# A two-layer graph network on one core: the prologue's folding and index work placed behind layer 0's table, three more superchunks gathered in place

## The chip, the cores and the metric

One Trainium2 chip, one of its cores. The metric is the device time of one execution in microseconds (us), the median of the runs. The engines are TensorE (PE, its weight loads PEld), VectorE (DVE), ScalarE (ACT), GpSimd (POOL) and SyncE (SP); "PEq", "SPq" and the like are their sequencers. The instructions of one engine stand in the trace in the order in which the program issues them.

## The reference, cut to what matters

6250 nodes with 256 features, 200,000 edges sorted by their destination. The features are normalized and cut at zero, run through two layers of graph attention (4 heads, then 1), and added to the input. One layer, in short:

```python
hx = (x @ Wg).reshape(n, h, f)
te = relu(edge_attr @ We + be) * exp(x @ Wo + bo)[src][:, None]   # edges, and a self loop of each node
he = (te @ Wge).reshape(-1, h, f)
al = leaky_relu((hx*a_s).sum(-1)[src] + (hx*a_d).sum(-1)[dst] + (he*a_e).sum(-1), 0.2)
al = exp(al - segment_max(al, dst)[dst])
al = al / segment_sum(al, dst)[dst]
out = segment_sum(hx[src] * al[:, :, None], dst) + b
```

Layer 0 is `relu(out + x)`, layer 1 `out + x`, and the result is the input plus all this.

## The kernel before, in words

**Tables and superchunks.** For each layer a table T in DRAM holds one row per node: hx, its two attention terms, the gate exp(x @ Wo + bo), and in layer 0 the two numbers of the node's normalization. The attention vectors are folded into the weights first (`fold`, lines 186 to 199; `fold_e`, lines 201 to 214, for the edges): TensorE turns a weight matrix, ScalarE copies it out of PSUM (line 183), TensorE multiplies it with the vectors (193, 208), VectorE copies the columns into the weights (197, 198, 210, 213). The edges go in 66 superchunks per layer, 64 of them of 24 chunks of 128 edges. A superchunk's source rows are gathered from T by 24 indirect DMAs, which POOL issues (line 941), into a buffer G of 128 x 24 x 270. VectorE makes logits, running maxima over each destination and weights, scales the rows (1303 in layer 0; ScalarE does it in layer 1, 1312), and TensorE sums them by destination with one-hot matrices (1322).

**Buffers.** Superchunk k takes the buffer k mod 3 as a new tile, whose first gather waits until the tile before in this place has been read entirely. The exception is superchunk 3: `own` (lines 692, 693) gives it superchunk 0's tile G0 itself, and each gather then waits for the readers of its own column only. Superchunk 0 has no gathers from T: its 24 columns of input rows are gathered from x during the prologue (line 274) and go through the same steps as the table's tiles.

**The prologue** (lines 218 to 439) makes layer 0's table in 49 tiles of 128 nodes (NT), in nine groups of 2, 5, 7, 7, 7, 7, 7, 5 and 2 (`g0` is 9), and then the 24 columns of superchunk 0 as groups 9 (6 columns) and 10 (18). The order of all work is written out by hand in one loop over k. In round k stand: `turn` of tile k+1 (two products with the identity on TensorE, line 342, a copy on ScalarE, 344), `norm` of tile k+3 (ScalarE, 336), up to four pieces of statistics by `step`, `keep` of tile k-1 (VectorE adds the bias and writes the row, 474), and `mult` of tile k (TensorE, 470). At the first norm of a group `drain` issues what its statistics still lack.

**Statistics** (`stats`, lines 283 to 325): per tile a bn_stats (291) and a bn_aggr (294) on VectorE, then per group variance plus epsilon (299), a first guess of the inverse root (301), minus half the variance (303), and three Newton steps, which VectorE makes in nine pieces or POOL in twelve instructions and three that write the result (307 to 324). Groups 3 to 9 use POOL.

**What else the rounds hold:** `more` loads layer 1's weights (round 5), the index loads (round 6) and the index work (`indices`, 476 to 573, and `index_group`, 629 to 675; 33 pieces, nearly all VectorE's, one every other round from round 17 and one each from 50), the folds at rounds 12 to 14 (edges, layer 0), 24 to 26 (layer 1) and 30 to 32 (edges, layer 1), and one gather of x in rounds 0 to 9 and in every fourth from 16. `idle` (254) multiplies the identity with itself, 128 x 512, and is used three times at the start. The group's rows go to T in `store` (357 to 362): two small ScalarE instructions and a DMA on SP's queue. Behind the last store `load_lb`, `load_ea` and `load_fl` issue superchunk 0's edge inputs; `lb` is a copy of `locrow`, which the index work writes to DRAM (520), and `fl` of `flags` (538).

**The edge loop** (`edges`, 678 to 774) starts with `nodes`, which loads rows of T and x into `tw`, then `gather`, `spread` (1065, 1066: it compares `lb`), `parts`, and the rest of superchunk 0.

**SP's queue.** The program gives the DMAs of SP and ScalarE eight semaphores in turn: a DMA is issued only when the one eight before it has landed, and all behind it on the queue wait with it.

Of the kernel before, what the change touches and what calls it, by code (L numbers as in the profile page):

```python
# [31 lines left out]
P = 128  # L32
# [47 lines left out]
class Kernel:  # L80
# [137 lines left out]
    def prologue(self):  # L218
# [7 lines left out]
        with ExitStack() as c:  # L226
# [56 lines left out]
            def stats(g):  # L283

                n, x = len(groups[g]), xs[g]
                w = GT if g < g0 else C
                st = wp.tile([P, w, 6], F32, name=f"st{w}", bufs=2 if g < g0 else 1)
                mv = wp.tile([P, w, 2], F32, name=f"mv{w}", bufs=3 if g < g0 else 1)
                s = wp.tile([P, 3, w], F32, name=f"sc{w}", bufs=3 if g < g0 else 1)
                for i in range(n):  # L290
                    V.bn_stats(st[:, i, :], x[:, i, :])
                    yield
# [12 lines left out]
                e = nc.gpsimd if 3 <= g <= g0 else V  # L305
# [59 lines left out]
            ahead = {g: stats(g) for g in range(1, len(groups))}  # L365
# [4 lines left out]
            def step(g):  # L370

                for q in list(ahead):
                    if q > g if q < g0 else k < (16 if q == g0 else NT):
                        continue
# [7 lines left out]
            for k in range(-3, len(tiles) + 1):  # L382
                if k == 6:
                    next(index)
                    gi = self.index_load(0, wp)
                    index = chain(index, self.index_group(0, wp, gi))
                if k > 16 and k % 2 or k > NT:
                    next(index, None)
                if k == 5:
                    more()  # L390
                if k == 8:
# [5 lines left out]
                if k in (12, 24, 30):  # L397
                    folds.append(fold(self.L[1], pt) if k == 24 else fold_e(self.L[k // 30], pt))
                    next(folds[0])
                if k in (14, 26, 32):  # L400
                    drain(folds.pop())
                if k == 26:
                    edge_weights(self.L[1])
                if 0 <= k + 1 < len(tiles):
# [10 lines left out]
                if 0 <= k - 1 < len(tiles):  # L415
# [7 lines left out]
                if 0 <= k < 10 or k >= 14 and k % 4 == 0:  # L423
                    next(rows0, None)
                if k == max(NT - 6, 7):
                    while not hasattr(self, "flags"):
                        next(index)
                    next(index)
                if 0 <= k < len(tiles):
                    mult(*tiles[k])  # L430
                while kept < g0 and groups[kept][-1] <= k - (3 if k < NT - 3 else 1):
                    store(kept)
                    kept += 1
                    if kept == g0:
                        self.load_lb(0)
                        self.load_ea(0)
                        self.load_fl(0)
# [240 lines left out]
    def edges(self, ctx):  # L678
# [13 lines left out]
        if len(steps) > 3 and steps[3]["L"].l == 0:  # L692
            steps[3]["own"] = self.G0
# [16 lines left out]
        for k, st in enumerate(steps):  # L710
# [13 lines left out]
            if st["s"] + 3 == self.NS:  # L724
                self.ending(st, *steps[k + 1:k + 3], pv, late, steps[k + 3] if k + 3 < len(steps) else None)
                pv = late = None
                continue
            self.gather(nx)
# [946 lines left out]
```

## Time and profile before

| | us |
|---|---|
| median of 3 runs | 4016.55 |
| lowest, highest | 4015.93, 4017.98 |
| the profiled execution | 4015.31 |
| its span, first to last instruction | 4013.5 |

| engine | busy us | share of the span |
|---|---|---|
| TensorE | 2655.2 | 66% |
| VectorE | 2446.4 | 61% |
| ScalarE | 1119.4 | 28% |
| POOL | 2998.9 | 75% |

A timeline row gives start, length, engine, line, operation, tiles written and read with their shapes, how many alike, and in brackets the idle time before with what ended it. A group's row gives the same with the sum of busy time, the mean length of one in ns, and the sum of the idle time before them. The DMA-issuing instructions of POOL are counted as busy.

### The profile page before, as it was taken

Reading aid. Unit: us, or ns where it says so; the run is one execution under the profiler, and the core shown is the slowest. Engines: PE = TensorE matmul, PEld = TensorE weight load, DVE = VectorE, ACT = ScalarE, POOL = GpSimd, SP = SyncE. Lnnn points to the kernel's source line nnn. Section 1 sums busy time; section 2 is a strip of 40 time slices with the busy share of each in tenths; the row PEclk is TensorE's granted clock in tenths of the full one; section 3 lists DMA queues with packets and bytes.
Section 4 is the critical chain, followed back from the end, with each engine's and each line's share of the span. In section 5 each row is a group of like instructions: output and inputs, shape, how many; then the busy total and the mean of one; then the engine's idle time right before and its main releaser. Section 6 shows DMA issues by size and latency. Waiting matters only on the chain.

```text
span 4013.5 us, 37615 instructions
## 1 busy us (share of the span) xinstructions
PE 2655.2 (66%) x9998; PEld 1744.1 (43%) x9998; DVE 2446.4 (61%) x6071; ACT 1119.4 (28%) x2676; POOL 2998.9 (75%) x3264
## 2 busy tenths in 40 slices
PE   8776766766766666666676566566665665665665
PEld 6454444444444444444454343343343343343343
DVE  7898877877877877877874443443443443443445
ACT  6211111111111111111124343343443443443441
POOL 6777777777777777777767777777777777777775
PEclk9888887788888888888888777777777777777777
DMA  7555555555555555555555445445445545545543
GB/s 245 141 160 151 145 154 144 150 154 144 152 154 145 150 154 144 151 155 143 152 155 145 133 138 143 134 137 145 137 134 143 139 132 144 138 132 143 140 131 94
DMA packets 240037, 584.66 MB, mean 146 GB/s; under 512 B 64843, under 2 KB 97265, under 8 KB 239579
## 3 DMA queue, kind: packets, MB, share of 16 engines
q0 software_dynamic: 150144, 422.75, 39.6%
q1 hardware_dynamic: 89133, 159.15, 12.4%
q8 instruction: 86, 1.41, 0.1%
q14 instruction: 130, 1.06, 0.1%
q10 hardware_dynamic: 544, 0.28, 0.0%
HBM read 544.19 MB, written 38.12 MB: 145 GB/s over the span
## 4 chain that ended last, share of the span: by engine, by line
POOL 32%; DVE 28%; issue 14%; PE 11%; ACT 9%; DMA 7%; DVEq 0%; SPq 0%; POOLq 0%; ACTq 0%
POOL G L941 31%; DVE G L1303 8%; ACT G L1312 7%; DMA G<-T,src 7%; PE y L1041 4%; PE u L1322 4%; DVE S L1132 4%; DVE lb L1065 2%; PE ps L470 1%; DVE m L1251 1%; ACT R L1042 1%; DVE rt L1181 1%; DVE al L1199 1%; DVE al L1197 1%; DVE fb L1212 1%
## 5 line engine op out<-in xcount | busy, mean ns | idle before, releaser
L941 POOL DMA_INDIRECT G<-T,src x3102 | 2945.2, 949 | 961.5 <-issue 910.7
L1322 PE MATMUL u<-G,S 128*128 128x270 f32 (+1 forms) x6252 | 1578.4, 415 | 193.3 <-DVE G L1293 190.1
L1322 PEld LDWEIGHTS u<-G,S 128*128 128x128 f32 x6252 | 1284.6, 207 | 487.5 <-DVE G L1293 217.0
L1312 ACT ACTIVATE G<-G,kw 128x256 f32<-128x256 f32 x1512 | 609.0, 497 | 0.0
L1042 ACT ACTIVATE R<-y,webd 128x1024 f32<-128x1024 f32 (+2 forms) x264 | 235.4, 892 | 1275.9 <-PE y L1041 791.4
L1219 PE MATMUL lf<-ident,fb 128*36 128x128 f32 (+1 forms) x132 | 49.6, 376 | 757.5 <-DVE fb L1212 755.6
L1195 DVE TENSOR_TENSOR G<-rt,G 128x96 f32<-128x96 f32 (+1 forms) x132 | 30.4, 230 | 804.7 <-DMA G<-T,src 804.3
L1303 DVE TENSOR_TENSOR G<-G,kps 128x6144 f32<-128x6144 f32 (+3 forms) x77 | 440.9, 5735 | 0.0
L1132 DVE TENSOR_TENSOR S<-kps,loc 128x3072 f32<-128x3072 f32 x132 | 437.7, 3316 | 4.6
L1041 PE MATMUL y<-ea,webd 64*128 64x256 f32 (+1 forms) x1056 | 391.1, 835 | 50.0 <-ACT R L1042 50.0
L1050 PE MATMUL zad<-R,wea 128*64 128x384 f32 (+1 forms) x1056 | 297.6, 704 | 158.6 <-ACT R L1042 158.3
L1219 PEld LDWEIGHTS lf<-ident,fb 128*36 128x36 f32 (+1 forms) x132 | 15.7, 119 | 798.0 <-DVE fb L1212 795.5
L1050 PEld LDWEIGHTS zad<-R,wea 128*64 128x64 f32 x1056 | 85.8, 183 | 420.9 <-ACT R L1042 338.9
L1327 ACT ACTIVATE U<-u 128x270 f32<-128x270 f32 (+1 forms) x132 | 51.8, 393 | 636.8 <-PE u L1322 636.8
L1354 DVE SCALAR_TENSOR_TENSOR mg<-U,mw 128x1 f32<-128x1 f32 x66 | 14.7, 223 | 281.2 <-ACT mw L1352 281.2
L1041 PEld LDWEIGHTS y<-ea,webd 64*128 64x128 f32 x1056 | 123.7, 286 | 122.4 <-ACT R L1042 68.4
L1285 DVE SCALAR_TENSOR_TENSOR G<-U,kw,G 1x257 f32<-1x257 f32 x62 | 29.5, 476 | 183.4 <-ACT G L1312 183.4
L470 PE MATMUL fin<-wg,h1T 128*128 128x260 f32 x264 | 127.6, 634 | 4.3 <-ACT h1T L1417 4.3
L1181 DVE STREAM_TRANSPOSE rt<-zad 128x768 f32<-128x768 f32 (+1 forms) x130 | 126.1, 970 | 4.4 <-PE zad L1167 4.4
L1153 PE MATMUL zad<-a,Q 128*128 128x12 bf16 (+1 forms) x132 | 25.9, 196 | 148.6 <-DVE a L1148 148.2
L1065 DVE TENSOR_TENSOR lb<-lb,kps 128x1536 bf16<-128x1536 bf16 (+1 forms) x68 | 113.0, 1661 | 0.0
L1427 ACT ACTIVATE t1row<-t1row 128x1 f32<-128x1 f32 x66 | 13.4, 203 | 347.1 <-DVE t1row L474 347.1
(225 smaller groups left out, 2303.2 us busy)
## 6 DMA issues: line engine op xcount, KB each, us to landing
G<-T,src POOLq DMA_INDIRECT x3102, 2.8
ea<-in_ea_dram SPq DMA_DIRECT2D x64, 768.0 KB
lb<-locrow SPq DMA_DIRECT2D x64, 384.0 KB
nd<-t1row SPq DMA_DIRECT2D x66, 225.8 KB
tw<-nd SPq DMA_DIRECT2D x66, 225.8 KB
tw<-T SPq DMA_DIRECT2D x66, 117.2 KB
T<-t1row SPq DMA_DIRECT2D x66, 113.8 KB
tw<-in_x_dram SPq DMA_DIRECT2D x66, 112.0 KB
```

The source lines that it names most:

```text
L470: self.nc.tensor.matmul(ps[:, :L.MW], hT[:, k, :], self.wg[L.l][:, k, :], start=(k == 0), stop=(k == 1))
L941: nc.gpsimd.indirect_dma_start(out=G[:, c, 0:L.TW], out_offset=None, in_=self.T[L.l][0:self.N, :], in_offset=bass.IndirectOffsetOnAxis(ap= ...
L1041: nc.tensor.matmul(y[:, i, :n], self.webd[l][r, :], ea[r, w], start=True, stop=True)
L1042: nc.scalar.activation(R[:, :, w], y[:, :, :n], AF.Relu, bias=self.be[l])
L1050: nc.tensor.matmul(st["zad"][i * PH:(i + 1) * PH, o], self.wea[l][0], R[:, i, w], start=True, stop=False)
L1065: V.tensor_tensor(lb[:, :, :n], lb[:, :, :n], self.k_part.unsqueeze(2).to_broadcast([P, i, n]), op=OP.is_equal)
L1132: nc.vector.tensor_tensor(st["S"][:, c0:c1, :], self.k_iota.unsqueeze(1).to_broadcast(w), self.loc[:, o + c0:o + c1].unsqueeze(2).to_broad ...
L1181: V.transpose(rv[:, :32 * c].rearrange("p (b n) -> p b n", b=2), z.rearrange("p (b n) -> p b n", b=2)[:, :, :16 * c])
L1219: self.nc.tensor.transpose(self.lf[0:e.shape[1], 1:P + 1], e, self.ident)
L1303: nc.vector.tensor_tensor(v, v, pw[:, c0:c1, :].unsqueeze(3) .to_broadcast([P, c1 - c0, H, L.F]), op=OP.mult)
L1312: self.nc.scalar.activation(v, v, AF.Copy, scale=st["w"][:, c:c + 1])
L1322: nc.tensor.matmul(st["u"][:, :L.W], S[:, i, :], G[:, i, 0:L.W], start=(j == 0), stop=(j == c - 1))
```

## The change

- The five identity products `idle(5)` stand in round 1, ahead of tile 2's turn.
- `stats` takes several groups at once: 7, 8 and 9 (thirteen tiles) share their Newton steps. POOL makes them for groups 2 to 7 instead of 3 to 9.
- The gathers of x beyond the first six come one in every other round, from the round after group 2's statistics are issued.
- Group 10's statistics may begin in round 45 instead of 49.
- The index loads move from round 6 to 20, `tw`'s from 8 to 23, `more` from 5 to 26. The index work begins in round 51, one piece per round; what is left is issued behind the last round.
- The three folds move to rounds 53, 56 and 61 (f = 4, 7, 12, counted from the table's end).
- The table's last rows are kept and stored first thing in round 49; `load_ea` follows there, `load_lb` and `load_fl` in round 61.
- Superchunks 3, 4 and 5 of layer 0 are gathered into the tiles of superchunks 0, 1 and 2 themselves.

```diff
@@ -280,16 +280,17 @@
             for _ in range(6):
                 next(rows0, None)
-            def stats(g):
-
-                n, x = len(groups[g]), xs[g]
-                w = GT if g < g0 else C
-                st = wp.tile([P, w, 6], F32, name=f"st{w}", bufs=2 if g < g0 else 1)
-                mv = wp.tile([P, w, 2], F32, name=f"mv{w}", bufs=3 if g < g0 else 1)
-                s = wp.tile([P, 3, w], F32, name=f"sc{w}", bufs=3 if g < g0 else 1)
-                for i in range(n):
-                    V.bn_stats(st[:, i, :], x[:, i, :])
-                    yield
+            def stats(*gs):
+
+                n, g = sum(len(groups[g]) for g in gs), gs[0]
+                w = GT if n <= GT else C
+                st = wp.tile([P, w, 6], F32, name=f"st{w}", bufs=2)
+                mv = wp.tile([P, w, 2], F32, name=f"mv{w}", bufs=3 if w < C else 2)
+                s = wp.tile([P, 3, w], F32, name=f"sc{w}", bufs=3 if w < C else 2)
+                for q in sorted(gs, key=lambda q: q == g0 - 1):
+                    for i in range(len(groups[q])):
+                        V.bn_stats(st[:, groups[q][i] - groups[g][0], :], xs[q][:, i, :])
+                        yield
                 for i in range(n):
                     V.bn_aggr(mv[:, i, :], st[:, i, :])
                     if i % 4 == 3:
@@ -302,7 +303,7 @@
                 yield
                 V.tensor_scalar(v, v, -0.5, None, op0=OP.mult)
                 yield
-                e = nc.gpsimd if 3 <= g <= g0 else V
+                e = nc.gpsimd if 2 <= g <= g0 else V
                 for _ in range(3):
                     e.tensor_mul(t, y, y)
                     if e is V:
@@ -362,7 +363,11 @@
                                   trow[:, :n, :])
             drain(stats(0))
-            ahead = {g: stats(g) for g in range(1, len(groups))}
+            q = max(g0 - 2, 2)
+            ahead = {g: stats(g) for g in range(1, q)}
+            ahead[q] = stats(*range(q, g0 + 1))
+            for g in range(g0 + 1, len(groups)):
+                ahead[g] = stats(g)
             for _ in range(3):
                 next(ahead[1], None)
             drain(folds.pop())
@@ -370,7 +375,7 @@
             def step(g):
                 for q in list(ahead):
-                    if q > g if q < g0 else k < (16 if q == g0 else NT):
+                    if q > g if q < g0 else k < NT - 4:
                         continue
                     try:
                         return next(ahead[q])
@@ -380,27 +385,36 @@
             index = self.indices(wp)
             kept = 0
             for k in range(-3, len(tiles) + 1):
-                if k == 6:
+                if k == 20:
                     next(index)
                     gi = self.index_load(0, wp)
                     index = chain(index, self.index_group(0, wp, gi))
-                if k > 16 and k % 2 or k > NT:
+                if k > NT + 1:
                     next(index, None)
-                if k == 5:
+                if k == 1:
+                    idle(5)
+                if k == 26:
                     more()
-                if k == 8:
+                if k == 23:
                     none = a["x"][N:N + 2 * P, :].rearrange("n d -> (n d)")
                     for i, e in ((0, 1), (M + 1, P)):
                         w = self.tw4[i:e].rearrange("p i w -> p (i w)")
                         n, m = w.shape
                         nc.sync.dma_start(w, none[0:n * m].rearrange("(p w) -> p w", w=m))
-                if k in (12, 24, 30):
-                    folds.append(fold(self.L[1], pt) if k == 24 else fold_e(self.L[k // 30], pt))
+                f = k - NT
+                if f in (4, 7, 12):
+                    folds.append(fold(self.L[1], pt) if f == 7 else fold_e(self.L[f // 12], pt))
                     next(folds[0])
-                if k in (14, 26, 32):
+                if f in (6, 9, 14):
                     drain(folds.pop())
-                if k == 26:
+                if f == 6:
                     edge_weights(self.L[1])
+                if f == 0:
+                    keep(*tiles[k - 1])
+                    while kept < g0:
+                        store(kept)
+                        kept += 1
+                    self.load_ea(0)
                 if 0 <= k + 1 < len(tiles):
                     turn(*tiles[k + 1])
                 if 0 <= k + 3 < len(tiles):
@@ -412,7 +426,7 @@
                     norm(g, i, t)
                 if k < NT - 1:
                     step(g + 2)
-                if 0 <= k - 1 < len(tiles):
+                if 0 <= k - 1 < len(tiles) and f:
                     keep(*tiles[k - 1])
                 if k >= NT - 1:
                     step(g + 2)
@@ -420,21 +434,19 @@
                 step(g + 2)
                 if t >= NT:
                     step(g + 2)
-                if 0 <= k < 10 or k >= 14 and k % 4 == 0:
+                if 2 not in ahead and k % 2:
                     next(rows0, None)
-                if k == max(NT - 6, 7):
+                if f == 12:
                     while not hasattr(self, "flags"):
                         next(index)
                     next(index)
+                    self.load_lb(0)
+                    self.load_fl(0)
                 if 0 <= k < len(tiles):
                     mult(*tiles[k])
                 while kept < g0 and groups[kept][-1] <= k - (3 if k < NT - 3 else 1):
                     store(kept)
                     kept += 1
-                    if kept == g0:
-                        self.load_lb(0)
-                        self.load_ea(0)
-                        self.load_fl(0)
             drain(rows0)
             drain(index)
@@ -689,8 +701,6 @@
         nc.vector.memset(self.lf[0:4, 0:1], -BIG)
         steps = self.steps
         self.state = {0: None, 1: None}
-        if len(steps) > 3 and steps[3]["L"].l == 0:
-            steps[3]["own"] = self.G0
         self.nodes(steps[0])
         self.gather(steps[0])
         if self.NS % 2:
@@ -725,6 +735,8 @@
                 self.ending(st, *steps[k + 1:k + 3], pv, late, steps[k + 3] if k + 3 < len(steps) else None)
                 pv = late = None
                 continue
+            if 3 <= k + 1 < 6 and nx["L"].l == 0:
+                nx["own"] = steps[k - 2]["G"]
             self.gather(nx)
             st["rows"] = st["L"].l
             drain(self.logits(st))
```

## The prediction

> **What bounds the kernel now.** First the page's head and two of its groups, then the view of line 941 alone (shortest, middle and longest duration in ns, first and last start).
>
> ```profile
> span 4013.5 us, 37615 instructions
> ```
> ```profile
> L941 POOL DMA_INDIRECT G<-T,src x3102 | 2945.2, 949 | 961.5 <-issue 910.7
> ```
> ```profile
> L1195 DVE TENSOR_TENSOR G<-rt,G 128x96 f32<-128x96 f32 (+1 forms) x132 | 30.4, 230 | 804.7 <-DMA G<-T,src 804.3
> ```
> ```profile
> L941 POOL DMA_INDIRECT G<-T,src x3102: 942/946/1195, 82.7 to 3981.5; - x194
> ```
>
> POOL issues 3102 gathers of table rows. (3981.5 - 82.7)/3101 is 1.257 us from one to the next: 0.95 busy and 0.31 idle (961.5/3102), which ends on "issue", on nothing that the profile shows. The edge work waits for them, 804.3 us before line 1195. So the time is 82.7 us to the first gather, 3101 steps, and 32.0 us of tail; the change touches neither step nor tail. It is worth what it moves the first gather by, and what it adds or takes in stalls of POOL, which can arise only while POOL is ahead of the edge work, in the first superchunks. Now POOL's timeline (start, length, instruction, idle time before it):
>
> ```profile
> 24.89 0.21 POOL L307 TENSOR_TENSOR sc<-sc 128x7 f32<-128x7 f32 x1 [0.81 <-DVE sc L301]
> ...
> 28.86 0.25 POOL L324 TENSOR_SCALAR ln<-sc 128x7 f32<-128x7 f32 x1
> ```
> ```profile
> 34.62 0.21 POOL L307 TENSOR_TENSOR sc<-sc 128x7 f32<-128x7 f32 x1 [4.26 <-DVE sc L301]
> ...
> 38.97 0.25 POOL L324 TENSOR_SCALAR ln<-sc 128x7 f32<-128x7 f32 x1
> 39.39 1.07 POOL L274 DMA_INDIRECT G<-in_x_dram,src  x1 [0.16 <-issue]
> ```
> ```profile
> 82.67 0.94 POOL L941 DMA_INDIRECT G<-T,src  x1 [6.84 <-issue]
> ```
>
> Newton steps (lines 307 to 324) and gathers of x (274) share POOL's queue; then POOL sits 6.84 until the table is stored. TensorE makes the table. On its timeline line 342 turns a tile, 470 multiplies it (tile 48, the last of the table, at 76.06; the first row is tile 2's turn, and TensorE has been free since tile 0's product, 10.5), and 181, 193 and 208 are the fold products.
>
> ```profile
> 13.51 0.44 PE L342 MATMUL pT<-ident,h 128*128 128x128 f32 x2 [2.92 <-ACT h L336]
> ```
> ```profile
> 26.89 1.07 PE L470 MATMUL ps<-wg,hT 128*128 128x266 f32 x4
> 27.79 0.38 PE L181 MATMUL pT<-ident,wge 128*128 128x128 f32 x2
> 30.07 0.61 PE L208 MATMUL ps<-att,hT 128*128 128x4 f32 x4 [1.89 <-ACT hT L183]
> ...
> 35.83 1.06 PE L470 MATMUL ps<-wg,hT 128*128 128x266 f32 x4
> ```
> ```profile
> 54.27 0.38 PE L181 MATMUL pT<-ident,wge 128*128 128x128 f32 x2
> ...
> 55.90 1.06 PE L470 MATMUL ps<-wg,hT 128*128 128x266 f32 x4
> ```
> ```profile
> 76.06 1.06 PE L470 MATMUL ps<-wg,hT 128*128 128x266 f32 x4
> ```
>
> A product takes 0.90 (26.89 to 27.79); with its turn a tile takes 1.12, the eighteen from 55.90 to 76.06 without a gap. So TensorE sets the table's pace, and what stops it counts. Its clock stands in the windows view (PEclk, after POOL's column):
>
> ```profile
> 11.30:14.70 3.40, 1.19 (x6) 1.02 (x7) 3.20 (x15) 1.85 (x5) 2.49 (x4) 1.00 1.01 404
> 14.70:18.10 3.40, 3.40 (x12) 2.65 (x10) 2.64 (x16) 1.51 (x5) 2.51 (x3) 0.51 1.02 402
> ```
>
> After a window that was 35% busy comes one at half clock, which loses 1.7.
>
> **The change up to the table's last tile.** *Taken away.* fold_e of layer 0 at tile 12, with group 3's late Newton steps: 26.89 to 35.83 is 8.94 for four tiles of 1.12, so 4.46. fold_e of layer 1: 55.90 - 54.27, less tile 30's turn of 0.22, 1.41. fold of layer 1, between tiles 23 and 24:
>
> ```profile
> 45.69 0.60 PE L181 MATMUL pT<-ident,wg 128*128 128x128 f32 x4
> 46.60 1.05 PE L193 MATMUL ps<-att,hT 128*128 128x2 f32 x8 [0.31 <-ACT hT L183]
> 47.52 0.31 PE L342 MATMUL pT<-ident,h 128*128 128x128 f32 x1
> ```
>
> 47.52 - 45.69 = 1.83. Together 7.70.
>
> *idle(5).* At 266 columns in 0.90 a product of 512 takes two pieces of 0.43 each; five take 4.3. Ahead of tile 2's turn they run from 10.5 to 14.8, where the turn could start at 13.5: 1.3 lost, 1.7 of half clock saved, gain 0.4. The Trainium skill ("TensorE: Matmul & The Clock Gate", the section on why this matters for your kernels) holds gaps of up to about 3 us harmless; by it the five products would be a plain loss of 1.3. The rows speak against it: a gap of 2.92 was enough.
>
> *Newton steps.* Fifteen POOL instructions take 24.89 to 29.11 = 4.22, or 4.60 (group 4); I take 4.36, nearer to the first. A gather of x behind them takes 0.16 + 1.07, one behind a gather what those of line 941 do: 1.25. Group 2's steps move to POOL. Their input leaves VectorE behind tile 2's row, which ends within 0.2 of where it does now, so at 17.8:
>
> ```profile
> 17.60 0.22 DVE L301 TENSOR_SCALAR sc<-sc 128x7 int32<-128x7 int32 x1
> ```
>
> POOL ends them at 22.15 (VectorE now does it by 20.1). On ScalarE a norm that waits for POOL looks so:
>
> ```profile
> 74.62 0.60 ACT L336 ACTIVATE h<-G,ln 128x256 f32<-128x256 f32 x1 [0.15 <-POOL ln L324]
> ```
>
> Behind norm 7 stand group 0's store (0.2) and tile 6's copy (0.4), and for that copy waits product 6: it starts at 23.4 and not at 14.8 + 5 x 1.12 + 0.22 = 20.6. 2.8 lost. From here POOL is narrow. Its queue is, in program order, Newton 2, two gathers, 3, three gathers, 4, three, 5, three, 6, five, then the joint steps of groups 7 to 9. From 17.8: six Newtons 26.2, sixteen gathers 20.0, and 1.5 in which POOL, free at 24.7, waits for group 3's input, which leaves VectorE behind tile 7's row at 26.2: 65.5. A round of 4.36 + 3.75 = 8.1 against seven tiles, 7.84, costs TensorE 0.3: 1.2 for groups 3 to 6. The joint steps have five gathers ahead of them. Tile 42 is due at 24.3 + 34 x 1.12 + 1.2 = 63.6; with norm and copy, 0.8, it comes at 66.3: 2.7 lost, and a window 70% idle puts the 3.0 left of the next at half clock: 1.5. Joining saves POOL two rounds of 4.36, but of the gathers that now stand behind them five to seven come ahead of them. A joint step is 13 wide, which the trace does not have; at worst it goes by width, 13/7 of 4.36, and tile 42 is 3.7 later still. The last two gathers of x stand behind it and end at 68, ahead of the statistics that read them.
>
> Sum: -7.70 - 0.4 + 2.8 + 1.2 + 2.7 + 1.5 = +0.1. Ends: without the three POOL losses 8.2 earlier; with the joint step by width 3.7 later.
>
> *Loads moved on SP's queue* (index loads to tile 20, layer 1's weights to 26): the store of group 3, the load of group 8 and the store of group 4 queue behind them. SP's own waits (for whom, total, times, longest):
>
> ```profile
> SPq L361 <- DMA drow<-in_drow_dram: 5.2, 1, 5.2
> ```
>
> Today SP holds a store for 5.2 until the longest of them has landed, and it will hold these three about as long; the buffers that they free or fill are touched again some 7 after their turn. I cost it at nothing; without that cover, up to 3. The loads themselves are wanted only behind the table.
>
> *Last store.* ScalarE's second piece of it ended at 78.78, 1.66 after tile 48's product (77.12):
>
> ```profile
> 78.59 0.19 ACT L360 ACTIVATE trow<-trow 128x2 f32<-128x2 f32 x1
> ```
>
> Ahead of turn 50 it comes sooner, but VectorE now has twelve of group 10's statistics queued before that row: about 1.2 after. Gain 0.5 (ends 0 and 1.5). From there to the first gather 3.89 as now (82.67 - 78.78). First gather: 82.67 + 0.1 - 0.5 = 82.3.
>
> **Behind the table.** Two rows of TensorE, two of VectorE:
>
> ```profile
> 89.31 0.69 PE L342 MATMUL pT<-ident,h 128*128 128x128 f32 x2 [6.59 <-ACT h L336]
> ```
> ```profile
> 110.53 1.96 PE L470 MATMUL ps<-wg,hT 128*128 128x266 f32 x8
> ```
> ```profile
> 94.14 0.20 DVE L658 TENSOR_SCALAR flpen<-gt 128x96 bf16<-128x96 f32 x1
> ```
> ```profile
> 113.17 1.75 DVE L1065 TENSOR_TENSOR lb<-lb,kps 128x1536 bf16<-128x1536 bf16 x1
> ```
>
> From tile 48's product to tile 72's, TensorE needs 35.4 now, 26.9 of it work, 6.59 the wait for group 10's statistics and 1.7 half clock. Now they start four tiles sooner, but fold_e of layer 0 at tile 53 has its ScalarE copy behind norm 55, which waits for them: idle about 5, then half clock 1.7, and the folds' 0.5 + 1.83 + 1.41. Sum 37.3, 1.9 more. The index work fits beside the tiles (a piece of 0.2 to 0.8 per tile on VectorE), but seven pieces of 0.2 stand after the last row: 1.6. Superchunk 0, whose first work is line 1065, starts 0.1 + 1.9 + 1.6 = 3.6 later, at 116.8.
>
> Does POOL feel it? Superchunk 3 is gathered into superchunk 0's buffer, row by row behind the sums:
>
> ```profile
> 138.72 11.21 PE L1322 MATMUL u<-G,S 128*128 128x270 f32 x48 [0.96 <-DVE G L1303]
> ```
> ```profile
> 143.35 1.01 POOL L941 DMA_INDIRECT G<-T,src  x1 [0.30 <-PE u L1322]
> ```
> ```profile
> 174.39 0.94 POOL L941 DMA_INDIRECT G<-T,src  x1 [0.87 <-PE fin L1415]
> ```
>
> The first row of that buffer is free at 139.2, 4.1 ahead. That falls to 4.1 - 3.6 - 0.4 = 0.1: no stall, no reserve. Superchunk 4 waited 0.57 (0.87 - 0.30) for the whole of superchunk 1; in place it can begin with the first sums, so this goes. What is late next is superchunk 6, which takes a whole buffer of a step long summed. Gathers in place start 1.26 apart instead of 1.25 (1.01 in the row above): 0.2 for each of superchunks 4 and 5.
>
> Sum: -0.4 - 0.57 + 0.4 = -0.5 (rounded). The profiled execution, 4015.3 with a span of 4013.5, would be 4014.8; the median shown, 4016.55, is 1.2 above it: **4016.0**, the same within what can be told.
>
> **Rivals.** *POOL is not narrow*: TensorE keeps the tiles' pace to the end, the table is stored 4.2 (joint steps in time) to 8.2 sooner, and superchunk 0 moves with it. For it: group 3's 4.22, and POOL's idle 4.26 before group 4 today. Against: sixteen gathers in the same queue. 4011.8 if the last wait goes. *The clock holds*: the gap of 2.7 at tile 42 brings no half clock, and everything is 1.5 sooner: 4014.5. The Trainium skill ("TensorE: Matmul & The Clock Gate", the section named above) would have it so. The two windows above speak against it: 65% idle was enough, and tile 42's would be 70%. *Superchunk 0 comes late* (slower): its index rows now go from VectorE (lrow, tiles 55 to 58) to DRAM (locrow) and back (lb) behind the table, and superchunk 0 opens with lb, then tw. lrow ends at about 96; with some 3 to 5 for a small store to land, lb is issued at about 102. SP then holds the load of fl until the flags have landed, and tw is queued behind it: about 106.5. lb took at most 9.6, issued 79.23, awaited by SP until 88.82:
>
> ```profile
> 79.23 0.59 SPq L966 DMA_DIRECT2D lb<-locrow  x1
> ```
> ```profile
> 88.82 0.32 SPq L1010 DMA_DIRECT2D tw<-in_x_dram  x1
> ```
>
> So lb lands by 112 and tw, at the same length, by 116, where they are wanted at 116.8 and 119. From there on each us is one of stall at superchunk 3, which has no reserve: landings of twice that length bring lb at 121 and tw at 126, which costs 7 to 9: 4025. *In place waits for the whole buffer*, so that the edit doesn't do what it says: superchunk 4 then waits the 3.6 + 0.4 as well, 4020; against it, superchunk 3 starts now while the sums run.
>
> **How the numbers follow.** Forecast 0.5 (4014 to 4018.5), POOL not narrow 0.2, the clock 0.1, superchunk 0 late 0.15, whole buffers 0.05. 4011 to 4021 leaves out the far ends of the first and the third rival. 0.2%, about what a measurement of this kernel can tell from no change, is 8.0: faster by that needs every POOL loss gone, 0.02; slower needs nearly the full price of a late superchunk 0, 0.05; same 0.93.
>
> **What would show it.** Line 941's first start near 82.3; ten records of line 256 before tile 2's turn and no half clock after; TensorE idle before turns 7 and 42 with POOL's Newton as the cause; line 1065 near 116.8; superchunk 3 starting on TensorE's heels; no 0.87 before superchunk 4. A first gather before 79, or a gap of POOL over 2 us at superchunk 2 or 3, would prove the sum wrong.

## The result, and the profile after

The changed kernel takes 4022.39 us (median of 20 runs, 4019.80 to 4024.42), the kernel before 4017.36 beside it (20 runs, 4013.26 to 4019.48): 5.0 more, ratio 1.0014 [1.0008, 1.002] (a kernel's time over that of the kernel before, in brackets the 95% interval; so below too). The loss is clear of the noise, but only 0.14%. The forecast was 4016.0, at most 4021.

The page of the changed kernel and the view of its gather line (941 is 953 now):

```profile
span 4019.6 us, 37645 instructions
...
L953 POOL DMA_INDIRECT G<-T,src x3102 | 2945.9, 950 | 972.2 <-issue 902.2
...
L1207 DVE TENSOR_TENSOR G<-rt,G 128x96 f32<-128x96 f32 (+1 forms) x132 | 30.3, 230 | 808.7 <-DMA G<-T,src 808.3
```
```profile
L953 POOL DMA_INDIRECT G<-T,src x3102: 942/946/1203, 84.2 to 3989.0; - x194
```

POOL bounds the kernel as before, with the same steps; the last gather comes 7.5 later (3989.0 for 3981.5) and the tail is 1.4 shorter. POOL's timeline tells where: first gathers of superchunks 1 to 4, and below the row of before that the prediction left out, superchunk 2's:

```profile
84.23 0.94 POOL L953 DMA_INDIRECT G<-T,src  x1 [12.40 <-ACT hT L345]
...
120.42 0.94 POOL L953 DMA_INDIRECT G<-T,src  x1 [6.18 <-issue]
...
150.42 1.00 POOL L953 DMA_INDIRECT G<-T,src  x1 [0.30 <-PE u L1334]
...
180.81 0.99 POOL L953 DMA_INDIRECT G<-T,src  x1 [0.30 <-PE u L1334]
```
```profile
113.35 0.95 POOL L941 DMA_INDIRECT G<-T,src  x1 [0.95 <-ACT G L355]
```

The first gather is 1.56 later (84.23 for 82.67). Superchunk 2 waits 6.18 where it waited 0.95: 5.23. Superchunk 4 no longer waits its 0.87: -0.57. That is 6.2 of the 7.5; the rest is spread over 3100 steps. So most of the loss is one wait, and the page calls it "issue". A gap of POOL over 2 us at superchunk 2 is the sign that the prediction itself named as proof against its sum. What ends there is on VectorE's timeline:

```profile
119.23 0.25 DVE L686 TENSOR_REDUCE bad<-gt 128x1 f32<-128x96 f32 x1
119.41 1.78 DVE L1077 TENSOR_TENSOR lb<-lb,kps 128x1536 bf16<-128x1536 bf16 x1
```

Line 686 is the last piece of index work, the last thing the prologue does; it ends at 119.48, and superchunk 2 starts 0.94 later (0.94 or 0.95 in e5, e6 and e9 below too). Before, the last product ended at 112.49 and superchunk 2 followed 0.86 later, 0.65 behind its turn: the wait was there, almost without length. (The row names line 355 on ScalarE, which ended only 0.04 ahead of it; behind the last product the distance is 0.86 in e4, e7 and e13 as well.) The reason lies in the program, and e1 tests it: the buffers of superchunks 1 and 2 are laid over the memory that the prologue gives back, the first over its tiles of x, the second over the end of these and over scratch tiles used to the last.

TensorE tells why the prologue ends later. In order: tile 7's turn and tile 6's product, tile 38's product, tile 42's turn, the table's last product (tile 48), the first fold, the last two products:

```profile
22.44 0.69 PE L343 MATMUL pT<-ident,h 128*128 128x128 f32 x2 [2.20 <-ACT h L337]
22.93 2.12 PE L482 MATMUL ps<-wg,hT 128*128 128x266 f32 x4
...
63.18 0.74 PE L482 MATMUL ps<-wg,hT 128*128 128x266 f32 x1 [2.08 <-DVE trow L486]
...
70.04 0.33 PE L343 MATMUL pT<-ident,h 128*128 128x128 f32 x1 [1.81 <-ACT h L337]
...
78.25 0.61 PE L482 MATMUL ps<-wg,hT 128*128 128x266 f32 x2
...
84.19 0.38 PE L181 MATMUL pT<-ident,wge 128*128 128x128 f32 x2
88.91 1.02 PE L208 MATMUL ps<-att,hT 128*128 128x4 f32 x4 [4.33 <-ACT hT L183]
...
115.50 1.96 PE L482 MATMUL ps<-wg,hT 128*128 128x266 f32 x8
```

Tile 48 stands at 78.25 (76.06 before), the last products at 115.50 (110.53).

Each experiment below is compared with the kernel before beside it, which took 4014.7 to 4017.8; in e12 to e14 the mean granted clock was 0.72 (elsewhere 0.79) and the kernel before took 4877 to 4885, so these three are compared with that alone.

### The profile page after: what moved, and what is told of

Read it like the earlier page. It is cut to its first block, busy times and chain, and to the rows that moved or that the text cites. A ratio compares the mean times of both kernels' runs of the same rounds, so it can differ in the third digit from the quotient of the medians.

```text
span 4019.6 us, 37645 instructions
## 1 busy us (share of the span) xinstructions
PE 2660.1 (66%) x10008; PEld 1744.1 (43%) x10008; DVE 2445.4 (61%) x6054; ACT 1119.4 (28%) x2676; POOL 2995.3 (75%) x3249
```

## The experiments

**Theory 1**: the time follows superchunk 2's first gather, which waits for the last user of the memory that it takes over, and so follows the prologue's end. **Theory 2**: superchunk 0's lateness is the cost, and would be paid at superchunk 3 just the same. **Theory 3**: the first gather counts, as the prediction's sum has it.

All in one table, from the timelines (starts in us; "sums" are superchunk 0's first, "profiled" is the time of the profiled execution, which the starts belong to, and "rest" is that time less superchunk 3's start):

| kernel | median | 1st gather | superchunk 2 | its wait | sums | superchunk 3 | profiled | rest |
|---|---|---|---|---|---|---|---|---|
| before | 4017.4 | 82.67 | 113.35 | 0.95 | 138.72 | 143.35 | 4015.31 | 3872.0 |
| changed | 4022.4 | 84.23 | 120.42 | 6.18 | 145.79 | 150.42 | 4021.40 | 3871.0 |
| e1 place | 4021.0 | 83.51 | 113.66 | 0.30 | 144.69 | 146.18 | 4016.84 | 3870.7 |
| e2 loads | 4022.3 | 83.07 | 119.81 | 6.67 | 145.18 | 149.80 | 4022.30 | 3872.5 |
| e3 loads, folds | 4017.8 | 83.42 | 114.30 | 0.30 | 139.07 | 144.38 | 4017.40 | 3873.0 |
| e4 loads, index | 4020.5 | 85.33 | 117.94 | 2.91 | 143.84 | 148.04 | 4019.54 | 3871.5 |
| e5 fold's round | 4020.2 | 84.13 | 116.09 | 1.26 | 141.09 | 146.10 | 4017.07 | 3871.0 |
| e6 Newton | 4017.9 | 79.76 | 116.91 | 6.81 | 142.29 | 146.91 | 4018.45 | 3871.5 |
| e7 in place | 4015.9 | 79.82 | 110.57 | 0.95 | 136.15 | 140.58 | 4012.45 | 3871.9 |
| e8 best | 4012.9 | 78.89 | 108.87 | 0.30 | 129.77 | 139.20 | 4013.73 | 3874.5 |
| e9 repairs | 4014.6 | 79.72 | 112.05 | 1.26 | 137.43 | 142.06 | 4014.16 | 3872.1 |
| e10 changed again | 4023.4 | 84.53 | 121.35 | 6.68 | 146.73 | 151.32 | 4022.82 | 3871.5 |
| e11 best, later fold | 4014.2 | 82.52 | 112.54 | 0.30 | 134.18 | 142.70 | 4015.50 | 3872.8 |
| e15 order, in place | 4013.0 | 80.33 | 110.34 | 0.30 | 131.66 | 140.48 | 4012.98 | 3872.5 |
| e16 order | 4013.0 | 80.22 | 110.23 | 0.30 | 131.55 | 140.39 | 4011.57 | 3871.2 |

The last column shows what counts: fifteen profiled executions over 11.3 us, and each takes superchunk 3's start plus 3870.7 to 3873.0, but for e8 (3874.5). The first gather alone does not tell it: e6, with its first at 79.76, took 1 longer than e3 with 83.42. The profiled execution is one of those that the median is taken of; in e1, e5 and e7 it was the fastest of them, so there the medians show less of a gain than the traces.

**e1, another place for superchunk 2's buffer.**

```diff
+            tp = self.pool("rows", 1, c)
             wp = self.pool("pw", 2, c)
-            trows = [wp.tile(...) for i in range(3)]
+            trows = [tp.tile(...) for i in range(3)]
```

> The changed kernel with the three tiles of table rows (trow) in a memory pool of their own, laid out right behind the tiles of x, so that superchunk 2's buffer comes to lie over tiles that are done with when the table is stored, and no longer over the prologue's other scratch tiles. Theory 1 (superchunk 2's first gather waits for the last user of the memory that its buffer takes over, VectorE's last piece of index work): the idle 6.18 before it falls to 0.3, superchunk 2 starts at 114.5; superchunk 3 then would start at 144.6 but waits for the first sums of superchunk 0 (start 145.8), so about 2.6 of the 5.9 comes back there: 4019.1, 3.3 less than the changed kernel's 4022.4. Theory 2 (superchunk 0's lateness alone is the cost and the wait at superchunk 2 only shows it sooner): all 5.9 comes back at superchunk 3: 4022.4. Theory 3 (it is the first gather that counts): 4022.4 as well, with no wait at superchunk 3.

Ratio 1.0009 [1.0, 1.0018]. POOL's rows of superchunks 2 and 3, and TensorE's first sums:

```profile
113.66 0.94 POOL L954 DMA_INDIRECT G<-T,src  x1 [0.30 <-ACT h L338]
...
146.18 0.94 POOL L954 DMA_INDIRECT G<-T,src  x1 [2.74 <-issue]
```
```profile
144.69 1.63 PE L1335 MATMUL u<-G,S 128*128 128x270 f32 x6 [0.95 <-DVE G L1316]
```

Nothing in the order of the work changed, and the 6.18 is gone: it was the memory. 2.74 comes back at superchunk 3 (2.6 forecast), which now waits for superchunk 0's sums. By the trace theory 1 holds; theory 2 has its true part there, for less than half; superchunk 3 starts 4.24 sooner, and the profiled execution is 4.6 shorter. The median is only 1.4 less and lies between the two theories (4019.1 and 4022.4); its interval, 3.6 either way, can't tell them apart.

**e2, the loads back on SP's queue; e3, the folds too; e4, the index work instead.**

```diff
-                if k == 20:      # index loads
+                if k == 6:
-                if k == 26:      # more()
+                if k == 5:
-                if k == 23:      # tw
+                if k == 8:
```

e3 has this and the folds' lines of the kernel before, e4 this and the index work's:

```diff
-                if f in (4, 7, 12):
+                if k in (12, 24, 30):
...
-                if f in (6, 9, 14):
+                if k in (14, 26, 32):
-                if f == 6:
+                if k == 26:
                     edge_weights(self.L[1])
```
```diff
-                if k > NT + 1:
+                if k > 16 and k % 2 or k > NT:
                     next(index, None)
```

> The changed kernel with the three loads that it moved on SP's queue (layer 1's weights, the index loads, tw's rows) back in rounds 5, 6 and 8; all else as changed. Theory 1 (the time follows the end of the prologue) with the cause of the late table in the load of x for group 8, which those loads hold up: VectorE's idle 6.36 ahead of group 8's statistics goes, TensorE's 2.08 and the half clock behind it go, the joint Newton steps come some 3 sooner but still late; first gather at 81.3 in place of 84.2, superchunk 2 at 117.5, time 4019.5. Rival (the joint Newton step of 13 tiles is late by POOL's own queue, and the load is hidden behind it): first gather at 83.5 or later, time 4021.7 or more.

> As the run before, and the three folds back at tiles 12, 24 and 30 as well. Their TensorE work moves from behind the table to ahead of its end: the first gather comes later (to about 85.8), while the end of the prologue moves only by what the folds cost behind the table, about 2 sooner than in the changed kernel. Theory 1 (the end of the prologue counts, through superchunk 2's first gather): about 4020.4, and superchunk 2 at 118.4. Theory 3 (the first gather counts, as the prediction's sum has it): 4024.0.

> The changed kernel with the three loads back in rounds 5, 6 and 8 and the index work back to one piece in every other round from 17; the folds stay behind the table. VectorE then has none of it left behind the last row. Theory 1: as with the loads alone, and the tail of 1.5 behind the last row goes too: superchunk 2 at 116.0, 4018.0. Theory 3 (the first gather counts): the same as with the loads alone, 4019.5, or later where the pieces get in the way of the table's rows.

Ratios 1.0012 [1.0003, 1.0021], 1.0002 [0.9993, 1.0011] and 1.0009 [1.0, 1.0018]. The loads do hold VectorE up in the changed kernel, here at group 8's statistics:

```profile
61.95 0.75 DVE L292 BATCH_NORM_STATS2 st<-x 128x6 f32<-128x256 f32 x2 [6.36 <-DMA x<-in_x_dram]
```

In e2 that idle is gone, but tile 42's turn waits all the same:

```profile
66.97 0.69 PE L343 MATMUL pT<-ident,h 128*128 128x128 f32 x2 [2.50 <-ACT h L337]
```

So the loads were worth 1.2 to 1.5 of the first gather (83.07 for 84.23 and, in e10, 84.53), not the 2.9 I expected, and the time is the rival's: POOL's queue was late by itself. e3 turned out better than expected: its first gather is hardly later (83.42), because TensorE's folds lie where it waits for POOL anyway (tile 42's wait is 0.16 there), and without them the prologue ends 6.0 sooner (tile 72's product at 109.76, in e2 115.79). With no wait at superchunk 2 it is within what can be told of the kernel before. In e4 the first gather comes 2.3 later than in e2, superchunk 2 1.9 and superchunk 3 1.8 sooner, and the median is 1.8 less, which the intervals can't tell apart: by the trace theory 3 has the sign wrong.

**e5, the first fold one round earlier.**

```diff
-                if f in (4, 7, 12):
+                if f in (3, 7, 12):
```

> The changed kernel with one number altered: the first fold of edge weights stands in round 52 in place of 53, so that its copy on ScalarE is queued ahead of the norm of tile 55, which waits for group 10's statistics, and no longer behind it. Theory (the fold's place in the queues cost the most: behind that norm it keeps TensorE from tiles 53 and 54 as well): the idle 4.33 ahead of line 208 goes, TensorE waits only at tile 55's turn, two tiles and the fold's products lie beside the wait, and the prologue ends 2 to 3 sooner: superchunk 2 at about 118, time 4020. Rival (the folds behind the table cost their own work and nothing else): superchunk 2 within 0.7 of 120.4, time 4022.4.

Ratio 1.0008 [0.9999, 1.0017]. TensorE around the fold, and superchunk 2:

```profile
82.88 0.38 PE L181 MATMUL pT<-ident,wge 128*128 128x128 f32 x2
83.80 0.61 PE L208 MATMUL ps<-att,hT 128*128 128x4 f32 x4 [0.53 <-ACT hT L183]
...
88.47 0.44 PE L343 MATMUL pT<-ident,h 128*128 128x128 f32 x2 [1.77 <-ACT h L337]
```
```profile
116.09 0.94 POOL L953 DMA_INDIRECT G<-T,src  x1 [1.26 <-issue]
```

One number moves the prologue's end by 4.3, and the profiled execution with it (the median by 2.2). In the changed kernel the fold's copy stood on ScalarE behind the norm of tile 55, which waits for group 10's statistics, and TensorE, in order, held tiles 53 and 54 behind the fold (4.33); ahead of that norm the fold waits 0.53, and what is left is 1.77 for tile 55, with no half clock behind it, as there was behind the 4.33.

**e6, group 2's Newton steps back on VectorE (with e2's loads).**

```diff
-                e = nc.gpsimd if 2 <= g <= g0 else V
+                e = nc.gpsimd if 3 <= g <= g0 else V
```

> As the run with the three loads back (e2_loads), and group 2's Newton steps back on VectorE, so that POOL makes them for groups 3 to 7 and the joint one. Against e2_loads: the idle of 2.2 ahead of tile 7's turn goes, with the half clock behind it (up to 1.1). Theory (POOL's queue sets the pace from its first Newton step on, so that all of it moves): the joint step and tile 42's wait come as late as before by the tile's own clock, the table is stored 2.2 to 3.3 sooner, first gather at 80, superchunk 2 at 117, time 4019. Rival (POOL's queue has a Newton step less, 4.4 of work, and is no longer narrow): tile 42's wait of 2.5 and its half clock go as well, first gather at 77, superchunk 2 at 114, 4016.5.

Ratio 1.0 [0.999, 1.0009]. Tile 42's turn and the first gather:

```profile
64.12 0.69 PE L343 MATMUL pT<-ident,h 128*128 128x128 f32 x2 [2.48 <-ACT h L337]
```
```profile
79.76 0.94 POOL L953 DMA_INDIRECT G<-T,src  x1 [13.86 <-ACT hT L345]
```

The theory's case by the trace: tile 7 no longer waits, everything comes 3 sooner (superchunk 2 at 116.91), and tile 42's wait keeps its length (2.48 for 2.50); the median, 4017.9, lies between the theory's 4019 and the rival's 4016.5. POOL is narrow from group 3 on, as the prediction said.

**e7, the kernel before with superchunks 3 to 5 in place, nothing else.**

```diff
-        if len(steps) > 3 and steps[3]["L"].l == 0:
-            steps[3]["own"] = self.G0
...
+            if 3 <= k + 1 < 6 and nx["L"].l == 0:
+                nx["own"] = steps[k - 2]["G"]
             self.gather(nx)
```

> The kernel before with only the last part of the change: superchunks 3, 4 and 5 gathered into the tiles of superchunks 0, 1 and 2. By the prediction's sum the 0.87 of idle ahead of superchunk 4's first gather becomes 0.3 and nothing else moves, -0.6, less than a median can tell. Rival (gathers in place start further apart): superchunks 4 and 5 take 0.2 more each and the gain is 0.2.

Ratio 0.9998 [0.9988, 1.0008]. Superchunk 4's first gather:

```profile
171.15 0.97 POOL L941 DMA_INDIRECT G<-T,src  x1 [0.30 <-PE u L1322]
```

The 0.87 is 0.30, and superchunk 5 takes 28.87 from its first to its last gather (28.80 before): no 0.2 each. Everything ahead of it is code of the kernel before, and yet its first gather is 2.85 sooner. The two windows of the prediction, in this run:

```profile
11.30:14.70 3.40, 1.47 (x8) 1.22 (x9) 3.23 (x14) 2.12 (x5) 2.49 (x4) 1.00 1.03 409
14.70:18.10 3.40, 3.40 (x21) 2.83 (x20) 3.12 (x21) 2.12 (x5) 2.50 (x3) 1.00 1.01 400
```

The gap ahead of tile 2 is 2.86, and no half clock follows (1.00); in the kernel before it was 2.92 and 0.51. Nor does any follow the fold at tile 12 here, with a gap of 2.36, as it did behind 1.89 in the kernel before. These two places make up 1.25 and 1.2 of the 2.85.

**e9, three repairs to the changed kernel, the diffs of e2, e5 and e6 together; e10, the changed kernel again, without an edit.**

> The changed kernel with the three repairs together that the runs so far point to: the three loads back in rounds 5, 6 and 8, group 2's Newton steps back on VectorE, the first fold of edge weights in round 52. If the repairs add up: first gather at 80 (as in e6_newton), the prologue's end 4.3 sooner than there (as the fold's round brought in e5_fold_round), superchunk 2 at 112.6, superchunk 3 at 142.9, no wait ahead of superchunk 4: 1 less than the kernel before, 4016.5. If they overlap (one wait behind all three), superchunk 2 stays at 116 or later and the time at 4018 or more.

> The changed kernel once more, unaltered, to see how far the prologue moves from one execution to the next. If the clock after a gap of TensorE is a matter of chance, the first gather differs from 84.2 by up to 1.5 and the half-clock windows stand elsewhere, while the two waits that carry the argument stay: TensorE held at the first fold by 4 or more, and superchunk 2 held until VectorE's index work ends, near 120. If the clock follows from the gap alone, every row up to 85 agrees within 0.2.

Ratios 0.9996 [0.9987, 1.0005] and 1.0017 [1.0007, 1.0027]. The repairs add up: first gather 79.72 (80 expected), superchunk 2 at 112.05 (112.6), superchunk 3 at 142.06 (142.9), 1.9 less than the kernel before beside it. So the three together account for the loss. e10 repeats the two waits (superchunk 2 at 121.35 behind 6.68; the product of tile 53 comes 7.1 behind the one before it), while the half clock behind the gap of 2.20 at tile 7 now covers other products.

**e8, a version built from this**: the kernel before with e1's place, the in-place gathers, and three moves in the prologue:

```diff
+                if k == NT:                      # last rows kept and stored first
+                    keep(*tiles[k - 1])
+                    ...
-                if k in (12, 24, 30):            # folds
+                if k in (12, NT + 2, NT + 3):
-                    ... k < (16 if q == g0 else NT)
+                    ... k < (16 if q == g0 else NT - 4)
```

> The kernel before with five parts that by the theory so far help: the tiles of table rows under superchunk 2's buffer (as in e1_place); superchunks 3 to 5 gathered in place; the table's last rows stored first in round 49; layer 1's two folds in rounds 51 and 52, ahead of the norm that waits for group 10's statistics, where TensorE idles 6.59; group 10's statistics allowed from round 45. Theory (POOL's start of superchunk 3 is the later of the first gather + 60.4 and superchunk 0's first sums + 1.5): the first gather 3.2 + 0.5 sooner, at 78.9, superchunk 0's sums no later than 138.7, superchunk 3 at 140 in place of 143.35, with the 0.6 before superchunk 4: 4.0 to 4.3 less than the kernel before, about 4013.2. Rival (POOL's Newton steps have no reserve either when TensorE is faster): the first gather stays above 81 and the gain is below 2: 4015.5 or more.

> The kernel of e8_best once more, unaltered, because its interval ended just under 1. If its gain is what the trace shows (superchunk 3 at 139 to 140 in place of 143.3, superchunk 4 without its wait: 4 to 5 us), the ratio lies near 0.999 again and the interval of the two together under 1. If it was a lucky prologue (the clock after TensorE's first gap moves the first gather by 1.5 either way), the first gather comes at 80 to 81 and the ratio near 0.9995.

> The kernel of e8_best once more. If its gain is what its trace showed, 0.999 of the kernel before with the first gather at 78.9 within 1.5, on a chip where the kernel before takes 4016 to 4018; if the chip is again one on which it takes 4885, the ratio there is again near 1.0085 and the loss belongs to that chip.

4012.9 (about 4013.2 expected), ratio 0.999 [0.9981, 0.9999], 4.9 below the kernel before beside it and 9.5 below the changed kernel's median. POOL's rows of superchunks 1 to 3:

```profile
78.89 0.94 POOL L947 DMA_INDIRECT G<-T,src  x1 [6.22 <-ACT h L337]
...
108.87 0.95 POOL L947 DMA_INDIRECT G<-T,src  x1 [0.30 <-ACT R L1048]
...
139.20 0.94 POOL L947 DMA_INDIRECT G<-T,src  x1 [0.30 <-issue]
```

POOL never waits there. Both repeats, e12 and e14, without an edit, came out with the low mean clock, and there the kernel loses: 1.0085 [1.007, 1.0099] and 1.0106 [1.009, 1.0122].

**e13 and e16, e8's prologue alone (e8 without the lines of e1 and e7); e15, e8 without the lines of e1.**

> The kernel before with only the parts of e8_best that move work inside the prologue: the last rows stored first in round 49, layer 1's folds in rounds 51 and 52, group 10's statistics from round 45. Superchunk 2's buffer lies where it lay and superchunks 4 and 5 take whole buffers. Theory (superchunk 2 waits for the prologue's end only if that is later than its turn): in e8_best the last product of the prologue stands at 102.4, 6 ahead of superchunk 2's 108.9, so the moved buffer did nothing there and superchunk 2 comes without a wait here too; only the 0.6 before superchunk 4 is lost: 0.999 of the kernel before, first gather 78.9, superchunk 3 at 139.2. Rival (the moved buffer is needed): an idle of over 1 ahead of superchunk 2.

> The kernel of e13_order_only, unaltered. Where the kernel before takes 4016 to 4018: first gather near 79, no wait ahead of superchunk 2, superchunk 4 with its wait of 0.9, 3.5 less than the kernel before, ratio 0.9991. If the in-place gathers carry the gain instead, 0.9998 or more.

> The kernel of e13_order_only (last rows stored first, layer 1's folds in rounds 51 and 52, group 10's statistics from round 45) with superchunks 3 to 5 gathered in place; superchunk 2's buffer stays where the kernel before has it. Theory (the moved buffer did nothing for the gain of e8_best): where the kernel before takes 4016 to 4018, the trace and time of e8_best: first gather near 79, no wait ahead of superchunk 2, ratio 0.999. On a chip where it takes 4880: superchunk 2 waits for the prologue's end near 141 as in e13_order_only, the ratio stays within 0.002 of 1, so that the 1% belongs to the moved buffer. Rival: the in-place gathers bring the 1% there.

e13, at the low mean clock, 0.9998 [0.9989, 1.0007]; e16 0.9994 [0.9985, 1.0003]; e15 0.9992 [0.9983, 1.0001]. In e15 and e16 no superchunk waits, with either buffers: the prologue's order carries the gain, the moved buffer nothing. That this order beats the kernel before rests on e8's interval; those of e15 and e16 just take in 1. At the low mean clock e13 and e14 differ by the moved buffer and the in-place gathers. Superchunk 2 in e13 waits for the prologue's end:

```profile
141.50 0.95 POOL L946 DMA_INDIRECT G<-T,src  x1 [22.50 <-ACT G L355]
```

In e14 it doesn't. Windows (busy PE, PEld, DVE, ACT, POOL, then PEclk) of e13 and of e14:

```profile
100.00:120.00 20.00, 5.14 (x12) 3.27 (x12) 1.21 (x5) 1.74 (x4) 14.43 (x16) 0.50 0.46 129
120.00:140.00 20.00, 16.95 (x78) 13.81 (x79) 6.37 (x18) 11.13 (x26) 0.00 (x0) 0.82 0.01 4
```
```profile
100.00:120.00 20.00, 5.76 (x14) 3.79 (x15) 1.16 (x5) 2.62 (x7) 15.12 (x17) 0.50 0.49 131
120.00:140.00 20.00, 4.51 (x12) 2.74 (x10) 0.77 (x2) 0.87 (x2) 15.12 (x17) 0.50 0.41 109
```

Beside POOL's gathers the other engines crawl in these windows; the wait stops POOL and lets the prologue finish. Superchunk 0's sums start at 167.53 in e13 and 199.22 in e14, superchunk 3 at 175.66 and 201.25. That far both kernels differ by the moved buffer alone, since superchunk 3 is gathered in place in both; these 25.6 are its part of the 42.4 between the two profiled executions, one of each kernel. Whether the in-place gathers have a share in the rest wasn't seen, since e15 came out with the usual clock.

**e11, e8 with layer 0's fold of edge weights behind the table as well** (and a second buffer for its weights).

```diff
-                if k in (12, NT + 2, NT + 3):
+                if k in (NT + 2, NT + 3, NT + 6):
```

> As e8_best, with the first fold of edge weights (layer 0's) behind the table too, in round 55, behind the two of layer 1. In e8_best superchunk 0's first sums (129.8) are 8 ahead of what superchunk 3 needs, so work can still be moved from ahead of the table's end to behind it. The fold at tile 12 costs 3.9 - 1.1 = 2.8 of TensorE's time and the stretch up to tile 14 another 1.1 at most. Theory (only the first gather counts while superchunk 0 has that reserve): the first gather 2.8 sooner, at 76.1, and the time 2.8 less than e8_best, 4010.1. Rival (POOL's Newton steps for group 3 end at 29.1 whatever stands at tile 12, and tile 14 waits for them): first gather at 77.5 or later, 4011.5 or more.

0.9995 [0.9986, 1.0004], first gather 82.52: the rival. TensorE, no longer held at tile 12, runs into POOL's Newton steps, 1.56 ahead of tile 35 and 1.76 ahead of tile 49 (e8: 0 and 0.99), and the half clock at tile 2 was longer. What is taken off TensorE ahead of the table's end buys nothing here beyond POOL's pace.

## Why the prediction was wrong, step by step

- **What bounds the kernel**: right. But "the time to the first gather" was the wrong handle: what counts is superchunk 3's start, and it has three bounds: the first gather + 60.3 (e8), superchunk 2, held by the prologue's end, + 30.0, and superchunk 0's sums + 1.5 (e1).
- **"Does POOL feel it?"**, the step that failed. It priced superchunk 3's buffer alone, with its reserve of 4.1, and left superchunk 2's out. Superchunk 2's first gather had no reserve: its row, with an idle of 0.95 where 0.30 is usual, stood in the trace. By the prediction's own numbers (the prologue's end at 116.8 and the gather 0.9 behind it, where its sum has 113.35 - 0.4) the wait would have cost 4.8 more, and the forecast been 4021. Measured: 5.23 more, and e1 takes it away.
- **The table's last tile**, forecast 76.2, measured 78.25. Newton 2: 4.0 for 2.8 (tile 8 at 26.59, due at 22.54), since half clock followed its gap too. The rounds: 0.75 for 1.2. Tiles 36 to 42: 6.1 for 4.2 (71.53 - 57.58 - 7.84); with the loads back (e2) they lose 4.0, so that the wait for POOL was sized right and the loads, which the prediction cost "at nothing", are the second term that failed: 2.1 here, 1.8 in e10. The joint step's width costs next to nothing: 65.00 to 69.35 is 4.35 for thirteen, where seven took 4.2. Of the 4.46 taken away at tile 12, 1.2 was half clock that e7, with the fold still there, doesn't have either: that part hung on the clock.
- **idle(5)**: taken where group 2's Newton steps are VectorE's in both, by tile 7's product: 21.99 in e6, 22.41 before (22.41 to 23.02 in e8, e11, e15 and e16), 0.4 as forecast; but 21.16 in e7, where the gap without the products cost no half clock, so a loss of 0.8. The sign hangs on the clock.
- **Last store**: 0.6 for 0.5, right in sum and partly by luck: ScalarE's piece ended 1.3 behind tile 48's product (1.2 forecast), 0.3 sooner than before, and the other 0.3 came between it and the first gather, 3.60 where the forecast kept 3.89.
- **Behind the table**: 38.2 (to tile 72's product, 116.40) for 37.3, tail 1.5 for 1.6: right in sum. That the fold's place cost 4.3 of it was in the forecast as a given and not questioned; e5 shows that it was one round's choice.
- **Superchunks 3 to 5 in place**: right for superchunk 4 (-0.57) and in going row by row (superchunk 4 begins at 180.81, before the last of superchunk 1's sums ends at 181.50); the 0.2 each is not there.
- **Rivals.** POOL not narrow: refuted by e6. Whole buffers: refuted by that start of superchunk 4. Superchunk 0 late by lb: its load was issued at 104.95, 3 later than the rival had it, but VectorE's line 1077 followed line 686 without a gap, so lb was not awaited. The time fell near that rival's side by another mechanism. The clock: below.

## What to carry to other kernels

Ask of every buffer's first use what memory it takes over and who was there last; an idle of 0.95 where 0.30 is usual is a wait without length, and it grows with whatever is put in front of it. Before work is moved behind a point, follow it through each in-order queue: a copy queued behind a waiting norm held TensorE for 4.3. Where several bounds lie within a few us, price each of them, and check on a second profile what a single one shows of the clock.

## What the runs showed of the chip

- **The length of a gap alone does not settle the clock after it.** At the usual clock six profiles have the start without `idle(5)`, with gaps of 2.80 to 2.92 ahead of tile 2; five were followed by some half clock, e7 by none. Where the half clock falls differs too: behind the gap of 2.20 at tile 7 it covers other products in e10 than in the same kernel's first profile. The Trainium skill ("TensorE: Matmul & The Clock Gate", the section "What's actually happening") says that the activity window runs freely and doesn't start with the kernel; the runs agree with that, though none shows the window itself. The prediction should have weighed this rule: the one on gaps, as it read it, has five of the six against it, and one execution could not tell that the sixth would come out otherwise.
- **In e12 to e14 the other engines starve beside POOL's gathers**: from 120 to 140 TensorE had 4.51 of 20 beside a busy POOL (15.12, e14), 16.95 beside one at rest (e13). Between their few instructions the profile shows "issue" and "remote". At the usual clock TensorE had 15.91 in the same window beside a POOL as busy (e16):

```profile
120.00:140.00 20.00, 15.91 (x48) 9.02 (x49) 18.43 (x33) 2.06 (x3) 15.20 (x16) 0.59 0.58 161
```

It is not so all the time: from 160 to 180 of e13 TensorE had 17.84 beside gathers of 11.95. And the low mean clock may be a mark of this and not its cause: from 60 to 80, ahead of the gathers from T, e13 and e14 have TensorE busy for 20.00 of 20 at a clock of 1.00, and the 0.50 stands where TensorE has little to do. What the engines wait for stays open.
